# Expert choice from tokens turned once: gate products in far attention, scales by way of memory

## The chip, the cores and the metric

The kernel runs on one core of a Trainium2 chip. The metric is the device time of one execution in microseconds. Engines are named as the profile does: PE (TensorE) multiplies matrices, PEld is its weight load, DVE (VectorE), ACT (ScalarE) and POOL (GpSimd) work on vectors, and SP (SyncE) issues most DMAs. [...]

## The reference, cut to what matters

The reference runs four layers on x of shape (4, 56, 56, 128). Layer 0 is neighbourhood attention with an MLP, layer 1 a convolutional recurrence, layer 2 full attention and a dense mixture of eight experts, layer 3 an attention by distance and an expert choice. The change touches layer 3:

```python
t = t + _L3_attn_ref(_ln_t(t), ...)     # attention by distance
t = t + _L3_ffn_ref(_ln_t(t), ...)      # expert choice

# inside _L3_attn_ref
scores = jnp.exp(-GAMMA * dist2)
attn = jax.nn.softmax(scores, axis=-1)
return jnp.einsum('bqk,bkd->bqd', attn, V)       # V = inputs @ Wv.T

# inside _L3_ffn_ref, E = 64 experts, K = 8 tokens for each
logits = jnp.einsum('bsd,ed->bse', x, gate_w) + gate_b
probs = jax.nn.softmax(logits, axis=1)           # over the tokens of an image
vals, idx = jax.lax.top_k(probs.transpose(0, 2, 1), K)
# the chosen tokens are gathered and pooled by their probability, go through
# two layers of their expert, and the result is added back to the chosen tokens
```

`_ln_t` subtracts each token's mean over 128 channels and divides by its deviation.

## The kernel before, in words

**Shapes.** An image has 3136 tokens. x of all four images stays in SBUF as 28 tiles of 112 tokens (P) by 128 channels. Four tiles are a group, so an image has seven groups (NG) of 448 tokens (GW).

**Layer 3's attention** (`FarAttention`, "far"). The kernel uses that the normalised tokens lie far apart, so that every score is the same and the attention adds the mean of the values to every token. For each group it normalises the tokens (`tokens`), turns them by four TensorE transposes and one copy by ScalarE that also sums the channels (`turned`), forms short queries and keys (`products`, `with_norms`), and when all groups are done it adds to x the mean of the turned tokens times Wv (`mean`, `add`). A large set of small products, the bounds (L1861, reduced at L1867 on VectorE or L1873 on ScalarE), proves that the tokens are far apart. A fallback computes everything where they are not (`decide`).

**Layer 3's expert choice** (`ExpertChoice`). `pieces` and `steps` do for each image: statistics of the new x, an inverse root of the variance (`root`, on VectorE by Newton's steps), a `store` of x and of the roots to a table in memory, from which chosen tokens are gathered later; then for each group `tokens` (four normalisations), `turned` (four transposes, L208, and a copy, L2322) and `logits` (one TensorE product of the gate's weights, L2327, a copy to `taken`, and the eight largest values of each row, L2332). Then `choose` takes the top eight values and their places (L2350, L2351), starts four indirect DMAs that gather the tokens, `marked` marks the chosen places and takes the exponentials, and `gather` and `pooled` form the pooled tokens. Images 0 and 2 use the lower 64 partitions, images 1 and 3 the upper 64.

**Layer 3's experts.** `experts` streams 32 "lots" of weights, 1 MB each, through nine buffers. Sixteen rounds of four experts do `first` (L2442), `turned` (L2455, L2463, L2470) and `second` (L2476). The result of a round goes to a tile `found` (L2482) with two buffers, and from there by four small DMAs to `outs` (L2489). A lot's next load is issued by SP when its buffer is free, in program order with those DMAs. `scatter` adds the weighted results to x and stores the output.

**What sets the order.** The long part of the kernel is layer 2's attention, `Attention.run`: 175 steps for each image, each a score product (L2066), an exponential (L2073) and a value product (L2149). All other layers' work is cut into pieces with an estimated cost each, and `Paced` hands out pieces between the attention's steps, in proportion to cost; `merged` mixes two lists by their shares of cost. A piece marked `apart` is the last of its list in its step. The first image's layer 3 work runs beside the third image's attention, that of images 1 and 2 beside the fourth's. For the fourth image the mixture and far attention of group g - 1 trail the attention of group g (`trail`, tiles with the suffix "t"); its last group and its expert choice come behind all attention, in an order written out by hand at the end of `layers_of_safe_scores`. There, `beside` puts bounds between the steps. POOL and ACT share the normalisation of the last tokens.

Of the kernel before, what the change touches and what calls it, by code (L numbers as in the profile page):

```python
# [126 lines left out]
EARLY_BOUNDS = 4  # L127
NB = W // 8
# [1571 lines left out]
class FarAttention:  # L1700
# [16 lines left out]
    def __init__(self, env, ctx, flow, work):  # L1717
        self.env, self.flow, self.work = env, flow, work
        nc, ins = env.nc, env.ins
        self.cp = cp = ctx.enter_context(env.tc.tile_pool(name="d_const", bufs=1, side="right"))  # L1720
        self.small = ctx.enter_context(env.tc.tile_pool(name="d_small", bufs=2, side="right"))

        self.even = ctx.enter_context(ExitStack())
        self.held = [
            stack.enter_context(env.tc.tile_pool(name=name, bufs=1, side="right"))
            for stack, name in ((ctx, "d_odd"), (self.even, "d_even"))
        ]


        norm = work.tile([128, GW], F32, tag="xnT_m", name="norm")[:, : 2 * 129]  # L1730
        norm = norm.rearrange("p (i c) -> p i c", i=2)
        nc.sync.dma_start(norm, ins["norm_channels"])
        self.norm = cp.tile([128, 2, 128], BF16, tag="norm16", name="norm16")
        nc.vector.tensor_copy(self.norm, norm[:, :, :128])
        self.one = cp.tile([128, 2, 1], F32, tag="one16", name="one16")
        nc.vector.tensor_copy(self.one, norm[:, :, 128:129])
        self.q_w = cp.tile([128, NR, 32], F32, tag="q_w", name="q_w")
        self.k_w = cp.tile([128, 32], F32, tag="k_w", name="k_w")
        nc.gpsimd.memset(self.q_w, 0.0)
        nc.gpsimd.memset(self.k_w, 0.0)  # L1740
        self.far = cp.tile([128, 1], F32, tag="far", name="far")
        self.half = cp.tile([128, 1], F32, tag="half", name="half")


        n = B * NG * (NR * NC + 1)
        self.found = cp.tile([128, n], F32, tag="found", name="found")
        nc.gpsimd.memset(self.found, 0.0)
        self.most, self.sums = 0, n

    def weights(self):  # L1750
# [25 lines left out]
        def of_values():  # L1776
            ps = flow.one([128, 512], "w_ps")
            nc.tensor.transpose(ps[:, :C], loaded("w_v", ins["L3_attn_Wv"]), env.ident)
            self.v_w = cp.tile([128, C], F32, tag="v_w", name="v_w")
            nc.vector.tensor_copy(self.v_w, ps[:, :C])  # L1780
# [13 lines left out]
    def image(self, b, spans, places="d"):  # L1794
# [4 lines left out]
        x = env.x[b]  # L1799
        held = {"q": {}}  # L1800
        pool = self.held[1 - b % 2]

# [75 lines left out]
        def mean():  # L1878
# [5 lines left out]
                v_ps[:P, :C], total.to_broadcast([128, P]), self.v_w, start=True, stop=True  # L1884
            )
            held["v"] = v = sp.tile([P, C], F32, tag="v", name="v", bufs=1)
            nc.vector.tensor_copy(v, v_ps[:P, :C])

# [8 lines left out]
        def of(span):  # L1897
            take, norm = span_norms(env, sp, b, span, places)

            def tokens(g):  # L1900
                held["xn"] = normal(
                    env, self.work, places, b, g, norm, span, places == "t" and g == NG - 1
                )

            return [costing(1.8 * len(span), take)] + sum([
# [3 lines left out]
                    costing(1.2, lambda g=g: with_norms(g), True),  # L1909
                ]  # L1910
# [307 lines left out]
class ExpertChoice:  # L2218
# [9 lines left out]
    def __init__(self, env, ctx, flow):  # L2228
# [24 lines left out]
        ]  # L2253
        self.fold = cp.tile([2 * EC, EC], F32, tag="fold", name="fold")
        nc.gpsimd.tensor_tensor(self.fold, env.ident[:, :EC], env.ident[:, EC:], ALU.add)
        self.lots, self.at = {}, 0

# [7 lines left out]
    def pieces(self, b, places="d"):  # L2265
# [5 lines left out]
        for g in range(NG):  # L2271
# [10 lines left out]
    def steps(self, b, places, norms_of):  # L2282
# [20 lines left out]
        def root(groups):  # L2303
            of = slice(groups[0] * GT, (groups[-1] + 1) * GT)
            mean2, var = moments(env, sp, f"c{len(groups)}", st[:, of, :])
            inverse_root(env, sp, var, rs[:, of])
            nc.vector.scalar_tensor_tensor(off[:, of], mean2, -0.5, rs[:, of], ALU.mult, ALU.mult)
# [25 lines left out]

        def store(groups):
            of = slice(groups[0] * GT, (groups[-1] + 1) * GT)
            rows_of = self.rows[b].rearrange("(t p) c -> p t c", p=P)
# [54 lines left out]
        def pooled():  # L2391
# [13 lines left out]
            logits=logits, choose=choose, marked=marked, weighed=weighed, gather=gather,  # L2405
# [3 lines left out]
    def experts(self, ctx, pool, units, others=()):  # L2409
# [6 lines left out]
            self.late.tile([2 * EC, C], F32, tag=f"out{i}", name=f"out{i}", bufs=1) for i in range(2)  # L2416
# [55 lines left out]
        def second(q):  # L2472
# [8 lines left out]
            found = self.late.tile([128, C], F32, tag="found", name="found")  # L2481
# [24 lines left out]
    def scatter(self):  # L2506

        env, nc, flow = self.env, self.env.nc, self.flow
        for pair in range(2):
# [4 lines left out]
            bias = self.late.tile([2 * EC, C], F32, tag="c_bias", name="c_bias")  # L2514
# [382 lines left out]
def layers_of_safe_scores(env: Env, f, soft):  # L2897
    with ExitStack() as ctx:
# [63 lines left out]
        def chosen(b):  # L2962
            return listed("far", held["choice"].pieces(b))

        def to_mixture():
# [3 lines left out]
            held["far"] = far = FarAttention(env, right, flow, held["choice"].work)  # L2969
# [36 lines left out]
        with tc.manual_schedule(  # L3006
# [5 lines left out]
            *tail, products, with_norms = held["tails"][-1]  # L3012
# [24 lines left out]
            beside("scalar", 1)  # L3037
            of["tokens"](0), of["tokens"](1), of["turned"](0), of["logits"](0)
            of["root"](late)
            of["store"](late)  # L3040
            of["turned"](1), of["tokens"](2), of["logits"](1), of["turned"](2), of["logits"](2)
            beside("scalar", 1)
            of["tokens"](3), of["tokens"](4), of["turned"](3)
            of["tokens"](5), of["logits"](3), of["turned"](4)
            of["tokens"](6), of["logits"](4), of["turned"](5), of["logits"](5)
            of["turned"](6), of["logits"](6)
            of["choose"]()
            beside("scalar", 2)
# [3 lines left out]
            beside("both", 6)  # L3052
# [84 lines left out]
```

## Time and profile before

| | us |
|---|---|
| median of 3 runs | 2458.79 (2456.23 to 2465.73) |
| the profiled execution | 2462.98 |
| its span | 2461.2 |
| PE busy | 2337.9 (95%) |
| DVE busy | 1816.2 (74%) |
| ACT busy | 1550.7 (63%) |
| POOL busy | 293.8 (12%) |

Busy shares are means over the whole span. In the slices of the page, a digit is a share in tenths, and "PEclk" is the clock granted to TensorE. A row of the timeline gives the start in us, the duration, the engine, the line of the kernel, the operation, and output and input tiles with their sizes; an idle time before it, with what ended it, stands in brackets. Matrix products in float32 appear as two instructions each.

A few durations that matter: the transposes of a group of tokens (L208) have a median of 0.26 us for one; a gate product of a group is 0.96 us at full clock and 1.76 us at half. The exponential over a whole row of tokens in the tail (L2369) takes 2.90 us, the search for the top values' places (L2351) 3.42 us and their marking (L2363) 3.41 us.

### The profile page before, as it was taken

What the parts mean: (1) busy time and instruction counts of PE and PEld (TensorE: products, weight loads), DVE (VectorE), ACT (ScalarE), POOL (GpSimd) and SP (SyncE); (2) the same over time, 40 slices, a digit from 0 to 9 for tenths busy, and PEclk for the clock granted to TensorE, in tenths of its full rate; (3) what the DMA queues carried; (4) which work ended last, traced back from release to release, by engine and by line L of the source; (5) the groups of instructions that cost most, each with busy time, mean ns of one, the idle gap of its engine ahead of it and who ended that gap; (6) DMA issues with size and microseconds to landing.
All of it is one profiled execution on the core that took longest, in us unless ns stands there. A gap on an engine that the chain in (4) does not pass through costs nothing.

```text
span 2461.2 us, 38767 instructions
## 1 busy us (share of the span) xinstructions
PE 2337.9 (95%) x14357; PEld 1258.2 (51%) x14357; DVE 1816.2 (74%) x4816; ACT 1550.7 (63%) x3346; POOL 293.8 (12%) x578
## 2 busy tenths in 40 slices
PE   6999999999999999999999999999999998998585
PEld 4777777775455555555554444445444443433134
DVE  5666899983997958799678777854788576776554
ACT  4999889875666646676332556575545566775553
POOL 4423363320000000000000000100000001011302
PEclk9999999999999999999999999999999997998578
DMA  5100000000000000000000010000000010100676
GB/s 124 36 8 2 2 2 2 2 2 9 1 1 1 1 1 0 1 1 1 12 1 0 1 27 1 5 1 1 1 1 1 1 27 5 27 5 1 184 297 206
DMA packets 65642, 61.42 MB, mean 25 GB/s; under 512 B 17048, under 2 KB 60915, under 8 KB 61348
## 3 DMA queue, kind: packets, MB, share of 16 engines
q1 hardware_dynamic: 64932, 57.80, 8.4%
q8 instruction: 115, 1.88, 0.3%
q0 software_dynamic: 512, 1.06, 0.2%
q14 instruction: 83, 0.68, 0.1%
HBM read 45.83 MB, written 12.90 MB: 24 GB/s over the span
## 4 chain that ended last, share of the span: by engine, by line
PE 63%; DVE 6%; ACT 2%; DMA 2%; issue 2%; POOL 1%; SPq 0%; DVEq 0%; POOLq 0%; ACTq 0%
PE s_ps L2066 20%; PE o_ps L2149 20%; PE y_ps L1574 7%; PE d_ps L1861 3%; PE xT_ps L208 2%; PE g_ps L1207 2%; DMA lot<-in_L_ffn_lots 2%; PE l_ps L2327 1%; PE y_ps L2090 1%; PE z_ps L2042 1%; PE q_ps L1825 1%; DVE found L1867 1%; PE l_ps L1534 1%; ACT xn L1693 1%; DVE gated L1587 1%
## 5 line engine op out<-in xcount | busy, mean ns | idle before, releaser
L2073 ACT ACTIVATE e<-s_ps 128x448 f32<-128x448 f32 x688 | 366.5, 541 | 491.8 <-PE s_ps L2066 486.1
L2066 PE MATMUL s_ps<-zT,xnT 128*128 128x448 f32 (+1 forms) x1400 | 649.4, 554 | 0.0
L2149 PE MATMUL o_ps<-e,keep 128*128 128x448 f32 (+1 forms) x1376 | 648.5, 554 | 0.0
L2149 PEld LDWEIGHTS o_ps<-e,keep 128*128 128x128 f32 (+1 forms) x1376 | 241.7, 190 | 217.8 <-issue 217.2
L2066 PEld LDWEIGHTS s_ps<-zT,xnT 128*128 128x128 f32 (+1 forms) x1400 | 241.1, 189 | 213.9 <-issue 193.5
L1873 ACT ACTIVATE d_ps<-d_ps,half 128x448 f32<-128x448 f32 (+1 forms) x376 | 227.2, 605 | 88.0 <-PE d_ps L1861 86.3
L1867 DVE TENSOR_REDUCE found<-d_ps 128x1 f32<-128x448 f32 x324 | 196.9, 619 | 77.6 <-PE d_ps L1861 75.7
L1574 PE MATMUL y_ps<-experts,xnT 128*112 128x512 f32 x448 | 217.0, 608 | 0.0
L1587 DVE TENSOR_TENSOR gated<-y_ps,gate 112x512 f32<-112x512 f32 x220 | 148.8, 686 | 35.5 <-PE y_ps L1574 33.0
L1593 DVE TENSOR_TENSOR gated<-gated 112x512 f32<-112x512 f32 x330 | 151.8, 467 | 3.5
L1861 PE MATMUL d_ps<-q_near,k_near 32*128 32x448 bf16 (+1 forms) x700 | 135.4, 374 | 15.6 <-ACT d_ps L1873 10.0
L208 PE MATMUL xT_ps<-ident,xn 112*128 112x112 f32 x672 | 117.8, 283 | 34.1 <-ACT xn L1693 26.0
L208 PEld LDWEIGHTS xT_ps<-ident,xn 112*128 112x128 f32 x672 | 80.4, 147 | 113.5 <-ACT xn L1693 58.9
L1673 POOL TENSOR_TENSOR g_rs<-var,exponent 112x4 f32<-112x4 f32 x17 | 17.9, 1053 | 1006.3 <-DVE var L1672 895.3
L1574 PEld LDWEIGHTS y_ps<-experts,xnT 128*112 128x112 f32 x448 | 77.2, 180 | 98.9 <-issue 63.8
L1861 PEld LDWEIGHTS <-k_near 32*128 32x128 bf16 (+1 forms) x700 | 32.0, 92 | 181.2 <-issue 167.2
L1693 ACT ACTIVATE xn<-x,g_off,g_rs 112x128 f32<-112x128 f32 x220 | 93.2, 486 | 26.3 <-DVE g_off L1675 13.0
L677 DVE TENSOR_TENSOR e<-e,band 112x1792 f32<-112x1792 f32 (+3 forms) x56 | 99.9, 1788 | 10.2 <-ACT e L670 10.2
L782 PE MATMUL f_ps<-w_fc,h 128*112 128x128 f32 x896 | 104.8, 274 | 1.9 <-ACT h L773 1.6
L782 PEld LDWEIGHTS f_ps<-w_fc,h 128*112 128x112 f32 x896 | 99.8, 177 | 5.2 <-ACT h L773 4.8
L768 PE MATMUL h_ps<-zT,w_fc 128*128 128x448 f32 x224 | 88.9, 540 | 0.6 <-ACT zT L762 0.6
L670 ACT ACTIVATE e<-s_ps 112x1792 f32<-112x1792 f32 (+3 forms) x56 | 82.6, 1476 | 6.3 <-PE s_ps L661 3.3
(427 smaller groups left out, 3939.7 us busy)
## 6 DMA issues: line engine op xcount, KB each, us to landing
lot<-in_L_ffn_lots SPq DMA_DIRECT2D x32, 1024.0 KB
out_x<-x SPq DMA_DIRECT2D x28, 224.0 KB
x<-in_x SPq DMA_DIRECT2D x3, 1568.0 KB
rows<-x SPq DMA_DIRECT2D x3, 1568.0 KB
x<-in_x SPq DMA_DIRECT2D x7, 224.0 KB
parts<-in_waves SPq DMA_DIRECT2D x8, 173.0 KB
out<-found SPq DMA_DIRECT2D x60, 2.0 KB
rows<-x SPq DMA_DIRECT2D x1, 896.0 KB
```

Source lines behind the costliest of these rows:

```text
L208: self.nc.tensor.transpose(ps[:, j * P : (j + 1) * P], xn[:, j, :], self.ident[:P, :P])
L782: nc.tensor.matmul(f_ps[:, j, :], h[:, k, j * P : (j + 1) * P], w_fc2[:, k, :], start=(k == 0), stop=(k == 3),)
L1574: nc.tensor.matmul(y_ps, held["xnT"][g][:, j * P : (j + 1) * P], self.experts[:, 4 * i : 4 * i + 4, :], start=True, stop=True,)
L1587: nc.vector.tensor_tensor(gated[:, some, :], y_ps, gate[:, some].unsqueeze(2).to_broadcast([P, 4, C]), ALU.mult,)
L1593: by.tensor_tensor(gated[:, :n, :], gated[:, :n, :], gated[:, n : 2 * n, :], ALU.add)
L1693: env.nc.scalar.activation(xn[:, j, :], env.x[b][:, g * GT + j, :], AF.Identity, bias=norm["off"][:, i : i + 1], scale=norm["rs"][:, i : i ...
L1861: nc.tensor.matmul(d, held["k"][part, 128 * c : 128 * c + n], held["q"][g][part, :], start=True, stop=True,)
L1867: nc.vector.tensor_reduce(self.found[:, self.most : self.most + 1], d, AX.X, ALU.max)
L1873: nc.scalar.activation(d, d, AF.Relu, bias=self.half[:n], accum_out=self.found[:n, self.sums : self.sums + 1],)
L2066: nc.tensor.matmul(s_ps[i * n : (i + 1) * n, :GW], self.xnT[:, at : at + n], zT, start=True, stop=True,)
L2073: nc.scalar.activation(e[:n], s_ps[:n, :GW], AF.Exp)
L2149: nc.tensor.matmul(sums[:, :GW], self.keep[:n, k, :], e[:n], start=(k == 0 and g - 1 not in pairs), stop=last,)
```

## The change: what it does, and the diff

The gate's product is taken from the tokens that far attention turns, so that expert choice needs no normalised and turned tokens of its own. The gate weights are centred once (`centre`), so a token's mean drops out. For each group, far attention's new piece `logits` multiplies the turned tokens by the gate weights and each column by the token's deviation, which gives the product of the unnormalised token. When the mean of the values is known, its gate product (`moved`, one number for each expert, from a widened `v_w`) is added, and the sum is multiplied by the inverse deviation of the new x.

Both factors stand in SBUF as one number per partition (token), and are needed as rows along the free axis, on 64 partitions. `keep_scales` stores them to memory with a DMA, and `fetch_scale` reads a group's row back to 64 partitions. For the very last group's deviations and all of the last image's inverse deviations, `spread` makes the rows on TensorE instead, from a broadcast column and the identity. Empty pieces with a cost (ROWS_COME) let other work come between a store and its first use. In the last image, all additions and statistics come ahead of the first gate work, and the inverse roots are a power on GpSimd.

To make room, `outs` and `c_bias` move into other tiles and `found` has one buffer. In the hand-written order, `beside` has other counts.

```diff
+ROWS_COME = 12.0
 # FarAttention
         def of_values():
+            self.choice.centre()
...
+            nc.tensor.matmul(ps[:, C : C + EC], w_v, self.choice.gate_w, start=True, stop=True)
-            self.v_w = cp.tile([128, C], F32, tag="v_w", name="v_w")
+            self.v_w = cp.tile([128, C + EC], F32, tag="v_w", name="v_w")
...
         def mean():
...
+            m_ps = flow.one([128, 512], "m_ps")
+            nc.tensor.matmul(m_ps[rows, :1], self.v_w[:, C:], total, start=True, stop=True)
+            nc.scalar.copy(choice.moved[b // 2][rows], m_ps[rows, :1])
...
+            def deviations():
+                held["sd"] = sd = sp.tile([P, n], F32, tag=f"g_sd{n}_{places}", name="g_sd", bufs=1)
+                nc.vector.reciprocal(sd, norm["rs"])
+                if not final:
+                    choice.keep_scales(b, 0, span, sd)
             def tokens(g):
...
+                if not final:
+                    choice.fetch_scale(row[rows], b, 0, g)
+            def logits(g):
+                cols, row = slice(g * GW, (g + 1) * GW), held["row"][rows]
+                if final:
+                    ps = flow.one([128, 512], "sd_ps")
+                    choice.spread(ps, rows, held["sd"])
+                    nc.scalar.copy(row, ps[rows, :GW])
+                l_ps = flow.one([128, 512], "l_ps")[rows, :GW]
+                nc.tensor.matmul(l_ps, choice.gate_w, held["xnT"], start=True, stop=True)
+                nc.vector.tensor_tensor(raw[:, cols], l_ps, row, ALU.mult)
 # ExpertChoice
+    def keep_scales(self, b, i, span, scale):
+        self.env.nc.sync.dma_start(
+            self.scales[b][i].rearrange("g (j p) -> p (g j)", p=P)[
+                :, span[0] * GT : (span[-1] + 1) * GT
+            ].unsqueeze(2),
+            scale.unsqueeze(2),
+        )
+    def fetch_scale(self, row, b, i, g):
+        self.env.nc.sync.dma_start(row, self.scales[b][i][g].partition_broadcast(EC))
+    def spread(self, ps, rows, scale):
+        for j in range(GT):
+            self.env.nc.tensor.matmul(
+                ps[rows, j * P : (j + 1) * P], scale[:, j : j + 1].to_broadcast([P, EC]),
+                self.env.ident[:P, :P], start=True, stop=True,
+            )
     # pieces: instead of tokens, turned, logits
+        for g in range(NG + 1 if from_raw else 0):
+            if g == 0:
+                first.append(costing(ROWS_COME, lambda: None))
+            if g < NG:
+                first.append(costing(0.1, lambda g=g: steps["fetched"](g)))
+            if g == 0:
+                first.append(costing(ROWS_COME / 4, lambda: None))
+            if g:
+                first.append(costing(1.4, lambda g=g: steps["moved"](g - 1)))
     # steps
+            if last:
+                nc.vector.tensor_scalar(var, var, 1e-5, None, ALU.add)
+                nc.gpsimd.tensor_tensor(rs[:, of], var, env.exponent[:P, : var.shape[1]], ALU.pow)
+        def moved(g):
+            cols = slice(g * GW, (g + 1) * GW)
+            part = taken[:, cols]
+            if last:
+                ps = flow.one([128, 512], "rs_ps")
+                self.spread(ps, rows, rs[:, g * GT : (g + 1) * GT])
+                nc.vector.scalar_tensor_tensor(
+                    part, part, self.moved[b // 2][rows], ps[rows, :GW], ALU.add, ALU.mult
+                )
+            else:
+                nc.vector.scalar_tensor_tensor(
+                    part, part, self.moved[b // 2][rows], held.pop(("scale", g)), ALU.add, ALU.mult
+                )
+            nc.vector.max(held["best"][rows, g * KT : (g + 1) * KT], part)
     # second
-            found = self.late.tile([128, C], F32, tag="found", name="found")
+            found = self.late.tile([128, C], F32, tag="found", name="found", bufs=1)
 # the order by hand
             each("statistics", late)
-            beside("scalar", 1)
-            of["tokens"](0), of["tokens"](1), of["turned"](0), of["logits"](0)
             of["root"](late)
             of["store"](late)
-            of["turned"](1), of["tokens"](2), of["logits"](1), of["turned"](2), of["logits"](2)
+            logits()
             beside("scalar", 1)
-            of["tokens"](3), of["tokens"](4), of["turned"](3)
...
+            each("moved", early)
+            beside("scalar", 2)
+            each("moved", late)
             of["choose"]()
-            beside("scalar", 2)
+            beside("scalar", 4)
             products()
             of["marked"]()
             with_norms()
-            beside("both", 6)
+            beside("both", 8)
```

## The prediction

> **What bounds the kernel now.** I read the page's shares and slices first, then TensorE in windows of 20 us, then the timeline of the tail, then the waits of the DMA queue.
>
> ```profile
> span 2461.2 us, 38767 instructions
> PE 2337.9 (95%) x14357; PEld 1258.2 (51%) x14357; DVE 1816.2 (74%) x4816; ACT 1550.7 (63%) x3346; POOL 293.8 (12%) x578
> PEclk9999999999999999999999999999999997998578
> ```
>
> TensorE is the bound up to about 2245 us. Behind that its share and its clock fall together and the time is a chain through all engines. One dent lies earlier, the "7" of the clock. In windows (busy PE, PEld, DVE, ACT, POOL, then clock, DMA share, GB/s):
>
> ```profile
> 2020.00:2040.00 20.00, 19.66 (x79) 8.21 (x77) 7.87 (x18) 17.14 (x45) 0.00 (x0) 1.00 0.08 1
> 2040.00:2060.00 20.00, 15.62 (x47) 6.31 (x47) 9.98 (x33) 13.66 (x35) 1.01 (x1) 0.65 0.00 1
> 2060.00:2080.00 20.00, 18.55 (x42) 6.23 (x41) 13.90 (x27) 13.19 (x28) 6.21 (x10) 0.75 0.06 14
> 2080.00:2100.00 20.00, 18.50 (x49) 6.89 (x49) 17.49 (x39) 8.36 (x21) 0.74 (x3) 0.91 0.00 0
> ```
>
> TensorE's timeline there, and of a calm place of the same work, image 0's choice:
>
> ```profile
> 2045.52 1.36 PE L2327 MATMUL l_ps<-zT,gate_w 128*64 128x448 f32 x2 [0.42 <-ACT zT L2322]
> 2049.55 0.45 PE L208 MATMUL xT_ps<-ident,xn 112*128 112x112 f32 x1 [2.67 <-ACT xn L1693]
> ...
> 1502.28 0.55 PE L208 MATMUL xT_ps<-ident,xn 112*128 112x112 f32 x4
> 1502.76 0.37 PE L1861 MATMUL d_ps<-q_near,k_near 32*64 32x448 bf16 x1
> ...
> 1504.01 0.96 PE L2327 MATMUL l_ps<-zT,gate_w 128*64 128x448 f32 x2
> 1504.91 1.02 PE L2149 MATMUL o_ps<-e,keep 128*128 128x448 f32 x2
> ```
>
> In the dent the choice of image 1 stands in a heap: in the kernel's built order 63 TensorE instructions, 24 transposes and five gate products among them, lie between two score products. They wait for ScalarE's normalised tokens, and the clock falls to half. At the calm place they are strewn among attention and nothing waits.
>
> The tail, from the last image's last gate product to the first expert product:
>
> ```profile
> 2319.48 1.76 PE L2327 MATMUL l_ps<-zT,gate_w 128*64 128x448 f32 x2 [0.68 <-ACT zT L2322]
> 2322.50 0.22 DVE L2350 MAX8 top<-best 64x8 f32<-64x56 f32 x1
> 2338.26 0.15 DVE L2383 TENSOR_TENSOR share<-share,c_got 128x4 f32<-128x4 f32 x1
> 2341.98 1.94 PE L2442 MATMUL h_ps<-lot,pooledT 128*32 128x512 f32 x8
> ```
>
> **The change, part by part.** The sum is made against the profiled execution (2462.98 us, its span 2461.2 with 1.8 around it), 4.2 above the median of 2458.79.
>
> 1. Transposes of images 0 to 2: 3 x 28 go. Four take 1502.28 to 1502.76, 0.48 us of TensorE's time, elsewhere 0.38; at 0.43 for four, 21 x 0.43 = -9.0. The gate products stay (one per group, now from the attention's tokens). ScalarE loses 84 normalisations and 42 copies, which were hidden.
>
> 2. The dent. Time less busy share times clock over the three windows from 2040: 20 - 15.62x0.65 = 9.8; 20 - 18.55x0.75 = 6.1; 20 - 18.50x0.91 = 3.2; together 19.1. In the built order of the changed kernel the longest heap in the last two images is 19 instructions, and the choice's new steps have no TensorE work before their sum. So -19 if all of it goes. Against it stand new waits. VectorE gets, for each of 21 groups, a product (0.69 at L1587's nearest row) and a sum with product (0.62, L2377's row). Over 1820 to 2240 its windows sum to 309 of 420 us, 73%; the 14 sums, 7 products there and the trail's 6 make it 77%. It also waits for rows: a row goes to memory and back, two transfers of 2.5 us (median to landing of the rows' stores), while only some 12 VectorE instructions (0.3 us each in these windows) stand between the root and its first use: 5.0 - 3.6, some 1.5 to 2 us, five times. SP's later stores and fetches queue behind that wait, all with a reader a group later. Bounds of it: nothing (23% of VectorE is free), or 10 us and another dip of 19. I take +6, nearer to nothing, since image 0's choice shows TensorE waiting for nothing at 18 of 20 us of VectorE. Together -13.
>
> 3. The last image's products for groups 0 to 5 move from the tail into attention, where TensorE is the bound: 1504.01 to 1504.91 is 0.9 each, 6 x 0.9 = +5.4. Their stores and fetches have a group of some 60 us each. The sixth's VectorE product, 0.7, lies ahead of the tail: +0.7. The mean's new product with one column and its copy are off the path.
>
> 4. The tail up to the top values. Until 2290.3 (three groups added and measured) nothing changes. Then, from before's rows: moments 1.9, late statistics 16 x 0.22 = 3.5, moments 1.0, last group's product 0.7: VectorE is free for sums at 2297.4. GpSimd's power takes 1.0 behind its additions (end 2291.8): early scales at 2293.4, late at 2297.8. TensorE's spread of a group, four products of 112 columns each, is not in the trace. L2327 streams the same 448 columns: 1.76 at this clock. Early ones 2293.4 + 3 x 1.76 = 2298.7; two pieces of bounds (four products) 1.3; late ones 4 x 1.76, to 2307.0; last sum 0.68 and maxima 0.64; top at 2308.4 instead of 2322.5: -14.1. Bounds: where the four products do not overlap, 0.77 each (x_total's row), 3.1 a group: -4.8. Where TensorE is at full clock, VectorE's 7 x 1.32 from 2297.4: -15.9. Here the Trainium skill ("TensorE: Matmul & The Clock Gate", Part 1: The HAM clock gate) speaks: about 3.4 us of sustained work bring the full clock. The spreads are such work, so by the rule -15.9; by the row (0.50 throughout 2280 to 2344, and 0.50 too from 2050 to 2058 with TensorE busy 7.81 of 8) -14.1. I take the row.
>
> 5. From the top to the experts: before 2338.26 - 2322.50 = 15.8. Two more pieces for both engines are two reductions, +1.2. ScalarE's two further pieces end as the marks do (2316), hidden; bare they cost 0.8 each. The gather waits for the rows' stores on GpSimd, whose DMA ends at 2315, the queue being full of lots:
>
> ```profile
> 2312.00:2316.00 4.00, 2.86 (x7) 0.95 (x6) 1.09 (x2) 2.31 (x5) 0.88 (x2) 0.50 0.99 64
> 2316.00:2320.00 4.00, 3.22 (x7) 1.24 (x8) 0.64 (x1) 1.11 (x3) 0.00 (x0) 0.50 0.00 0
> ```
>
> Gathers from 2315.5, four in 5.2 and 2 to land: 2322.7, ahead of VectorE at 2308.4 + 17.0 = 2325.4. So it no longer has 12 us of cover but 2.7. Experts begin 14.1 - 1.2 = 12.9 earlier. The first nine lots are there since 2303, so all behind moves: -12.9.
>
> 6. "found" gets one buffer instead of two: VectorE's copy of a round now waits until the last round's four transfers have landed, and the next bias addition stands behind it. SP's waits and the last copies before:
>
> ```profile
> SPq L2489 <- DMA lot<-in_L_ffn_lots: 23.4, 15, 2.1
> ...
> 2415.00 0.29 DVE L2482 COPY found<-o_ps 128x128 f32<-128x128 f32 x1 [0.91 <-PE o_ps L2476]
> 2418.65 0.29 DVE L2482 COPY found<-o_ps 128x128 f32<-128x128 f32 x1
> 2421.36 0.28 DVE L2482 COPY found<-o_ps 128x128 f32<-128x128 f32 x1
> 2423.96 0.29 DVE L2482 COPY found<-o_ps 128x128 f32<-128x128 f32 x1 [1.26 <-PE o_ps L2476]
> ```
>
> While lots stream, seven rounds (2363.24 to 2410.07) take 6.7 us each, by DMA, and SP is held by landed lots already: nothing. In the last three rounds nothing streams: copy 0.3, semaphores 0.2, three issues of 0.54, landing 2.5 make 4.7 a round, 14.1 instead of 8.96: +5.1. Bounds: 0 and the slow rival below.
>
> Sum: -9.0 - 13 + 5.4 + 0.7 - 12.9 + 5.1 = -23.7. 2463.0 - 23.7 = 2439.3 profiled; less 4.2, a median of 2435.
>
> **The rivals.** (a) The dent moves instead of going: ScalarE still has far attention's seven groups within 13 attention steps[...]. For it speaks that the dip came from such a wait; against it the shorter heaps. Without the -13: 2448. (b) Slower: the single "found". If its transfers land only behind the two lots requested ahead of them (2 x 2.65, from 1 MB at some 395 GB/s), a round is 4.7 + 5.3 = 10.0 instead of 6.7, 13 times: +43, in place of the 5.1: 2473. It decides from 1.8 us a round. SP's wait for lots speaks for it; against it, that two lots requested in the last round keep the DMA fed meanwhile. (c) Rows come late in several places and the clock dips once more: +20, 2455. (d) All goes well: no new waits, full clock in the tail: -6 - 1.8, 2427. (e) That the DMA stores hide the tail's gain: the gather would have to start 2.7 later than reckoned; only some us of it, inside the range.
>
> **How the numbers follow.** Forecast 0.45, (a) 0.20, (b) 0.10, (c) 0.10, (d) 0.15. The likeliest one's own range is 2428 to 2445 (bounds of 4 and 6). 2424 to 2457 leaves out (b) and some 5 in 100 more. 0.5% is 12.3 us, about what a measurement can tell: below 2446.5 lie the forecast, (d) and two fifths of (a), 0.67; above 2471.1 (b), 0.10 and a little; the rest 0.22.
>
> **What would show it.** Step 2: clock 1.0 in all windows from 1400 to 2240, no wait of TensorE over 2 us there; a dent anywhere is (a) or (c). Step 1 and 3: attention's end some 16 us earlier. Step 4: the top values 23 us after the first addition to x (2285.4 to 2322.5 now, 37); a group's spread 1.8 us. Step 5: gathers not the last thing the share waits for. Step 6: copies of found 4.7 apart at the end and not over 7 in the middle. A round near 10 us, or a second clock dip, would make it wrong.

## The result, and the profile after

The changed kernel takes 2518.62 us (median of 4 runs, 2516.18 to 2521.87) where the kernel before took 2457.51 in the same comparison: 1.0242 of it, with an interval of 1.0216 to 1.0268. The forecast was 2435 and its range ended at 2457. The profiled execution has a span of 2520.0, 58.8 more than before. Its page:

```profile
span 2520.0 us, 38685 instructions
PE 2350.6 (93%) x14321; PEld 1258.7 (50%) x14321; DVE 1831.5 (73%) x4856; ACT 1492.6 (59%) x3203; POOL 292.5 (12%) x566
PEclk9999999999999999999999989999999998989787
```

TensorE's busy time hardly moved (2337.9 before), but its share fell and the clock has more dents. The stages say where. Starts are taken from the timelines: VectorE's first addition to x, the top values (L2350 before, L2462 after), the first expert product (L2442, L2555) and the first store of the output.

| stage, us | before | after | difference | forecast by the steps |
|---|---|---|---|---|
| start to the first addition | 2285.4 | 2351.7 | +66.3 | -15.9 (steps 1, 2 and 3) |
| first addition to top values | 37.1 | 21.3 | -15.8 | -14.1 (step 4) |
| top values to the first expert product | 19.5 | 21.2 | +1.7 | +1.2 (step 5) |
| experts, to the first output store | 88.1 | 94.5 | +6.4 | +5.1 (step 6) |
| rest | 31.1 | 31.3 | +0.2 | 0 |

The last four stages behave as forecast. The whole error, 82 us of it, lies in the long part ahead of the tail. There I added, in windows of 4 us from 1180 to the first request for lots (2279.1 and 2345.4), TensorE's busy share times its granted clock ("work", in us at full clock) and what is missing of the time ("lost"):

| | first lots | work | lost |
|---|---|---|---|
| before | 2279.1 | 1054.1 | 44.9 |
| after | 2345.4 | 1054.6 | 110.8 |

So TensorE has as much to do as before, and 66 us more are lost in waits and at half clock. Windows of the changed kernel at image 0's choice and in the place of the old dent (busy PE, PEld, DVE, ACT, POOL, then clock, DMA share, GB/s):

```profile
1488.00:1492.00 4.00, 4.00 (x14) 1.72 (x14) 3.34 (x9) 2.32 (x6) 0.00 (x0) 1.00 0.91 8
1492.00:1496.00 4.00, 2.04 (x7) 0.63 (x6) 0.00 (x0) 0.73 (x2) 0.00 (x0) 1.00 1.79 1
1496.00:1500.00 4.00, 0.00 (x0) 0.00 (x0) 0.00 (x0) 0.00 (x0) 0.00 (x0) 0.66 1.31 1
1500.00:1504.00 4.00, 0.00 (x0) 0.00 (x0) 0.00 (x0) 0.00 (x0) 0.00 (x0) 0.50 0.36 57
1504.00:1508.00 4.00, 2.46 (x4) 0.94 (x4) 3.86 (x7) 0.72 (x2) 0.00 (x0) 0.50 0.08 29
...
2060.00:2080.00 20.00, 10.71 (x39) 4.07 (x38) 3.29 (x19) 6.72 (x17) 1.01 (x1) 0.85 1.25 2
2080.00:2100.00 20.00, 13.28 (x47) 4.99 (x47) 12.57 (x33) 9.23 (x27) 0.00 (x0) 0.72 0.29 29
```

From 1496 to 1504 all five engines stand still. Up to 1500 the DMA engines are busy and move next to nothing: 1 GB/s. The timeline of the same place names the chain:

```profile
1487.65 0.18 DVE L925 SCALAR_TENSOR_TENSOR c_rs<-newton,guess 112x28 f32<-112x28 f32 x1
1487.85 0.31 SPq L2310 DMA_DIRECT2D scale<-c_rs  x1
1488.20 1.87 SPq L2450 DMA_DIRECT2D rows<-c_rs  x1
1499.19 6.09 SPq L2319 DMA_DIRECT2D scale<-scale  x3
1504.14 0.68 DVE L2438 SCALAR_TENSOR_TENSOR taken<-taken,moved,scale 64x448 f32<-64x448 f32 x1 [12.73 <-DMA scale<-scale]
1505.47 0.53 PE L1870 MATMUL d_ps<-q_near,k_near 32*128 32x448 bf16 x1 [11.43 <-DVE gated L1588]
```

The roots' store is issued at 1487.85; SP can issue the first load only at 1499.19, 11.3 us later, and the row is there at 1504.14. (A second store of single elements, that of the roots to the table of x, is under way with it.) VectorE stands before its sum for 12.73 us, and TensorE 11.43 us for a product of VectorE's (L1588) that stands behind that sum in the program and begins at 1504.74. The rows of the waits from 1200 to the tail (total us, times, longest):

```profile
DVE taken L1934 <- DMA row<-scale: 36.7, 5, 17.3
DVE taken L2438 <- DMA scale<-scale: 24.8, 2, 12.7
PE d_ps L1870 <- DVE taken L1934: 20.0, 2, 15.9
PE d_ps L1870 <- DVE gated L1588: 16.5, 5, 11.4
PE d_ps L1870 <- DVE found L1876: 12.4, 3, 8.8
```

Before, from 1400 to 2245, TensorE's longest wait for VectorE was 1.2 us:

```profile
PE d_ps L1861 <- DVE gated L1587: 2.5, 6, 1.2
```

VectorE waits 61.5 us for rows: 24.8 at two of the three choices, 36.7 at five products of far attention. Some 40 us of TensorE's waits in these rows stand behind that (20.0, 11.4 and 8.8); the other 8 or so stand behind waits for pooled tokens from GpSimd. In the windows of the table above, TensorE's idle time grew from 25.0 to 75.0 us, and what its busy time lost by a lower clock from 20.0 to 35.8. These two make the 66 us.

The tail, from the addition to the experts:

```profile
2351.69 0.69 DVE L1904 TENSOR_TENSOR x<-x,v 112x512 f32<-112x512 f32 x1
...
2358.64 2.28 POOL L2388 TENSOR_TENSOR c_rs<-var,exponent 112x12 f32<-112x12 f32 x1 [0.52 <-DVE var L2387]
2360.97 4.09 PE L2324 MATMUL rs_ps<-ident,c_rs 112*64 112x112 f32 x24 [3.17 <-POOL c_rs L2388]
...
2366.87 3.25 PE L2324 MATMUL rs_ps<-ident,c_rs 112*64 112x112 f32 x32 [0.35 <-ACT d_ps L1882]
...
2373.00 0.22 DVE L2462 MAX8 top<-best 64x8 f32<-64x56 f32 x1
...
2390.43 0.17 DVE L2495 TENSOR_TENSOR share<-share,c_got 128x4 f32<-128x4 f32 x1 [0.36 <-DMA c_got<-rows,c_at]
...
2394.16 1.94 PE L2555 MATMUL h_ps<-lot,pooledT 128*32 128x512 f32 x8
```

### The profile page after: what moved, and what is told of

The parts are those of the page before. It is cut to its first block, busy times and chain, and to the rows that moved or that the text cites. A ratio compares the mean times of both kernels' runs of the same rounds, so it can differ in the third digit from the quotient of the medians.

```text
span 2520.0 us, 38685 instructions
## 1 busy us (share of the span) xinstructions
PE 2350.6 (93%) x14321; PEld 1258.7 (50%) x14321; DVE 1831.5 (73%) x4856; ACT 1492.6 (59%) x3203; POOL 292.5 (12%) x566
## 3 DMA queue, kind: packets, MB, share of 16 engines
q1 hardware_dynamic: 90468, 63.40, 11.6%
## 4 chain that ended last, share of the span: by engine, by line
PE 57%; DVE 6%; DMA 6%; issue 3%; ACT 2%; POOL 2%; SPq 1%; DVEq 0%; POOLq 0%; ACTq 0%
PE s_ps L2101 18%; PE o_ps L2184 18%; PE y_ps L1575 7%; PE d_ps L1870 3%; PE g_ps L1208 2%; DMA scale<-g_sd 2%; PE xT_ps L209 2%; DMA out<-found 1%; DMA row<-scale 1%; DVE found L1876 1%; PE y_ps L2125 1%; PE z_ps L2077 1%; PE l_ps L1933 1%; PE l_ps L1535 1%; PE q_ps L1834 1%
## 5 line engine op out<-in xcount | busy, mean ns | idle before, releaser
L2101 PE MATMUL s_ps<-zT,xnT 128*128 128x448 f32 (+1 forms) x1400 | 660.8, 561 | 0.0
L2184 PE MATMUL o_ps<-e,keep 128*128 128x448 f32 (+1 forms) x1376 | 656.5, 559 | 0.0
L1588 DVE TENSOR_TENSOR gated<-y_ps,gate 112x512 f32<-112x512 f32 x220 | 148.6, 685 | 30.6 <-PE y_ps L1575 29.0
L1870 PEld LDWEIGHTS <-k_near 32*128 32x128 bf16 (+1 forms) x700 | 32.9, 92 | 239.9 <-issue 218.9
L1594 DVE TENSOR_TENSOR gated<-gated 112x512 f32<-112x512 f32 (+1 forms) x330 | 149.9, 463 | 2.2
L1674 POOL TENSOR_TENSOR g_rs<-var,exponent 112x4 f32<-112x4 f32 x17 | 17.3, 1017 | 1121.0 <-DVE var L1673 988.5
L209 PE MATMUL xT_ps<-ident,xn 112*128 112x112 f32 x560 | 93.3, 277 | 25.5 <-ACT xn L1694 16.9
L678 DVE TENSOR_TENSOR e<-e,band 112x1792 f32<-112x1792 f32 (+3 forms) x56 | 99.9, 1787 | 11.4 <-ACT e L671 11.4
L209 PEld LDWEIGHTS xT_ps<-ident,xn 112*128 112x128 f32 x560 | 64.6, 144 | 78.6 <-ACT xn L1694 38.2
```

Of the source, the lines that this page charges most:

```text
L209: self.nc.tensor.transpose(ps[:, j * P : (j + 1) * P], xn[:, j, :], self.ident[:P, :P])
L678: nc.vector.tensor_tensor(es, es, bands[stripes[i][1] == 0][:n].rearrange("p h r c -> p h (r c)").unsqueeze(2) .to_broadcast([n, NH, m, 8 ...
L1588: nc.vector.tensor_tensor(gated[:, some, :], y_ps, gate[:, some].unsqueeze(2).to_broadcast([P, 4, C]), ALU.mult,)
L1594: by.tensor_tensor(gated[:, :n, :], gated[:, :n, :], gated[:, n : 2 * n, :], ALU.add)
L1870: nc.tensor.matmul(d, held["k"][part, 128 * c : 128 * c + n], held["q"][g][part, :], start=True, stop=True,)
L2101: nc.tensor.matmul(s_ps[i * n : (i + 1) * n, :GW], self.xnT[:, at : at + n], zT, start=True, stop=True,)
```

## Experiments

Theory A: the stores of scales land slowly, because they consist of single 4-byte elements, and that alone makes the loss. Theory B: the order of the plan, or VectorE's additional work, makes it. Theory C: the single buffer of `found`. Theory D came up later: the place of the stores in the plan. The two measurements of stores (m_stores, m_strides) are one run each.

**Stores measured by themselves (m_stores).** In the kernel before, chains of one store (or two) and one dependent load:

```diff
+        forms = [
+            [turned("near0", N)], [turned("far0", N, 129)], [turned("line0", N, 16)],
+            [within("within0")], [lines("lines0")], [turned("few0", 7)],
+            [turned("near1", N), turned("far1", N, 129)],
...
+                nc.sync.dma_start(out, source)
+            nc.sync.dma_start(a, probe[:384].partition_broadcast(64))
```

> The kernel before, with 18 stores or pairs of stores put behind the choice of image 0, at a place where the DMA queue of SyncE has nothing else to do for 500 us. Each is followed by a load of 64 rows of 384 numbers that has to wait for it, and the next store waits for that load, so the times at which they are issued give the landing of each. Theory A (a store of single 4-byte elements is slow to land, and that is what the prediction had too small): 3136 elements at neighbouring addresses take about 10 us, two such stores together 16, 28 lines of 448 bytes about 2.5, 448 single elements about 6; a load about 4 to 5. If the neighbourhood of the addresses is what is slow, 3136 elements at 516 or 64 bytes from each other take 2.5 to 4 us; if it is the number of elements, they take 10 too. Theory B (the stores land in 2.5 us as the prediction had it, and the queue or the plan makes the rows late): all forms about 2.5 us. The time of the kernel stays that of the kernel before within 10 us.

Three of the eighteen in the timeline of SP's queue (neighbouring addresses, 516 bytes apart, lines); the distance from a store (L2294) to the load behind it (L2295) is the landing:

```profile
1190.37 0.68 SPq L2294 DMA_DIRECT2D near<-probe  x1
1208.36 0.52 SPq L2295 DMA_DIRECT2D probe<-in_x  x1
1211.17 0.63 SPq L2294 DMA_DIRECT2D far<-probe  x1
1217.06 0.47 SPq L2295 DMA_DIRECT2D probe<-in_x  x1
...
1233.92 0.36 SPq L2294 DMA_DIRECT2D lines<-probe  x1
1235.62 0.47 SPq L2295 DMA_DIRECT2D probe<-in_x  x1
```

| store (first, second time) | landing, us |
|---|---|
| 3136 single elements, neighbouring addresses | 18.0, 16.8 |
| 3136 single elements, 516 bytes apart | 5.9, 5.9 |
| 3136 single elements, 64 bytes apart | 6.8, 6.6 |
| 64 runs of 196 bytes | 1.7, 1.7 |
| 28 lines of 448 bytes | 1.7, 1.3 |
| 448 single elements, neighbouring addresses | 8.3, 8.0 |
| neighbouring and 516 apart, one behind the other | 21.8, 21.5 |
| two with neighbouring addresses | 28.4, 27.4 |
| two with 516 apart | 10.0, 10.0 |

A load took 2.7 to 2.9, once 4.3. So both count: being single elements costs about 4 us over lines, being neighbours another 11 to 12. That is more than the 10 us expected, in this shape of 64 partitions by 49 elements. Windows of half a us show where the time lies. For the second store of each kind, the DMA engines' last packets in the profile end at about 1340.5 with 516 bytes, 2.7 us before the landing at 1343.24; as neighbours they end at about 1324, 10.4 us before the landing at 1334.43. So most of what closeness costs comes behind the last packet that the profile shows. The kernel itself took 2487.72, 26 over before and not within 10: the built program put the stores at 1190 to 1440, and up to 1228 SP issues loads of attention weights among them. That these loads came late is likely, but not shown; the second half of the measurement has none of them.

**What distance is near (m_strides).** The same in the changed kernel's shape, with other distances:

```diff
+        forms = [
+            [across(f"across{s}", s)] for s in (1, 2, 4, 8, 16, 32, 129)
+        ] + [
+            [within("within2", 2)], [within("within4", 4)],
+            [across("few1", 1, 4)], [across("few16", 16, 4)],
+        ]
```

> The kernel before with stores put in as in the first measurement, now in the changed kernel's own shape, 112 partitions by 28 single elements (3136), each followed by a load of 112 rows of 384 numbers that waits for it. Elements of one partition lie 448 bytes or more from each other and neighbours come from neighbouring partitions (across), at 4, 8, 16, 32, 64, 128 and 516 bytes; or neighbours come from one partition (within), at 8 and 16 bytes. Theory A1 (stores of several partitions that fall into the same 64 bytes hinder each other): across takes about 10 us at 4 bytes, falls to about 6 at 64 and stays there; within takes about 6 at 8 and 16 bytes. Theory A2 (any write close behind another one into the same 64 bytes is slow, whoever makes it): within at 8 and 16 bytes takes as long as across at the same distance. 448 elements: 6 to 8 us at 4 bytes, 2.5 at 64. The time of the kernel is 15 to 30 us over that of the kernel before, since loads of weights queue behind the measured stores.

| 112 x 28 single elements | landing, us |
|---|---|
| neighbours from other partitions, 4 bytes apart | 12.0, 11.7 |
| 8 bytes | 8.3, 7.5 |
| 16 bytes | 6.1, 6.4 |
| 32, 64, 128 bytes | 5.5 to 5.9 |
| 516 bytes | 6.2, 6.3 |
| neighbours from one partition, 8 bytes apart | 16.5, 17.3 |
| neighbours from one partition, 16 bytes apart | 14.3, 13.6 |
| 448 elements, 4 bytes apart | 6.9, 8.0 |
| 448 elements, 64 bytes apart | 1.7, 1.8 |

A1 falls: neighbours from one partition are not faster but twice as slow as neighbours from several at the same distance. A2 has the direction (any write close to another is slow) but not the size. That writes which follow each other closely in one queue are the worst would fit; it was not tested. The kernel took 2478.95.

**The form of the store in the kernel (e_turned).**

```diff
     def keep_scales(self, b, i, span, scale, place="d"):
-        self.env.nc.sync.dma_start(
-            self.scales[b][i].rearrange("g (j p) -> p (g j)", p=P)[...].unsqueeze(2),
-            scale.unsqueeze(2),
-        )
+        nc.tensor.transpose(ps[:n, :P], scale, self.env.ident[:P, :P])
+        nc.scalar.copy(lines[:n], ps[:n, :P])
+        nc.sync.dma_start(
+            self.scales[b][i].rearrange("g (j p) -> (g j) p", p=P)[...], lines[:n],
+        )
```

The stores became pieces of their own in the plan, 4 cost units behind the root.

> The changed kernel, with one thing other: the scales are turned on TensorE and stored as lines of 448 bytes, not as single elements (12 more products of 112 columns, each 4 cost units behind the root). Theory A (trip of the stores): a trip of 16 us becomes 7, VectorE's waits for rows fall from 61 us to under 20, and with them the falls of the clock: 2518 becomes about 2445 to 2465. Theory B (the order of the plan, or VectorE's additional work, costs the time): 2505 to 2520. Theory C (the single buffer of found): no change, 2515 to 2520.

2447.15 us, 0.9937 of the kernel before (0.9921 to 0.9954). Work 1060.6 and lost 36.0 ahead of the first lots at 2276.6. SP's waits for the stores' landing, in the changed kernel

```profile
SPq L2319 <- DMA scale<-g_sd: 69.3, 9, 10.0
SPq L2319 <- DMA scale<-c_rs: 18.0, 2, 9.1
```

and in this one, with what is left of VectorE's waits for rows:

```profile
SPq L2328 <- DMA scale<-lines: 17.8, 11, 6.6
DVE taken L2449 <- DMA scale<-scale: 7.7, 3, 5.7
```

SP's wait for a store fell from 7.9 us to 1.6, and VectorE's waits for rows from 61.5 us to 7.7. Theory C and the additional work of B fall: the single buffer and that work are still there. The order of B is left.

**Two controls (e_back, e_split).** In the kernel with lines VectorE has 32, 6 and 34 instructions between the root and the choice's first sum, against 10, 9 and 13. So the order has moved along with the form. The first control keeps this order and stores single elements; the second stores single elements straight from their tiles, with the plan's pieces as in the kernel with lines.

```diff
 # e_back, against e_turned
+        nc.tensor.transpose(back_ps[:P, :n], lines[:n], self.env.ident[:n, :n])
+        nc.scalar.copy(lines[:P, :n], back_ps[:P, :n])
         nc.sync.dma_start(
-            self.scales[b][i].rearrange("g (j p) -> (g j) p", p=P)[...], lines[:n],
+            self.scales[b][i].rearrange("g (j p) -> p (g j)", p=P)[...].unsqueeze(2),
+            lines[:P, :n].unsqueeze(2),
         )
```

> A control for the kernel with lines of 448 bytes, in which the stores lie elsewhere in the plan too, so that VectorE has 32, 6 and 34 instructions between the root and the choice's first sum, where the changed kernel has 10, 9 and 13. Here the scales are turned into lines, turned back on TensorE and stored as single elements from there: the instructions of VectorE stand as in the kernel with lines (32, 6 and 34), the store is that of the changed kernel. Theory A (the store's landing): the trip is 8 us longer in each of 12 places, VectorE's waits for rows come back to 35 to 60 us, and the time is 2480 to 2510. Theory D (the place in the plan brought the gain, and not the form of the store): 2447 to 2455.

> The other control: the changed kernel with the stores of single elements straight from their tiles, as pieces of their own in the plan, 4 cost units behind the root, as in the kernel with lines. VectorE has 10, 3 and 16 instructions between the root and the choice's first sum. Theory A: as slow as the changed kernel within 15 us, 2500 to 2525. Theory D: 2447 to 2465.

e_back: 2572.95 us, 1.0456 (1.0438 to 1.0474). e_split: 2519.27 us, 1.0242 (1.0225 to 1.0259), the changed kernel's own time. So neither the new order nor the new place in the plan brings the gain without the lines: D falls, and with it what was left of B. Waits of e_back, then of e_split:

```profile
SPq L2331 <- DMA scale<-lines: 113.4, 12, 13.4
ACT xn L1695 <- DMA scale<-lines: 67.1, 8, 19.0
DVE taken L2452 <- DMA scale<-scale: 45.4, 8, 14.4
```

```profile
DVE taken L2444 <- DMA scale<-scale: 50.4, 5, 22.7
DVE taken L1937 <- DMA row<-scale: 16.8, 5, 6.1
```

With the same order of VectorE's instructions a store takes 9.5 us of SP's time (113.4 in 12) instead of 1.6, and VectorE waits 45.4 for rows instead of 7.7. e_back is beyond its expected 2510: the lines lie in the buffer of the next normalised tokens, so that ScalarE waited too, 67.1 us, which was not reckoned. So its direction counts, and its size does not. What the lines alone bring in the changed kernel's own order (10, 9 and 13) was not run; where the order with lines has only 6 instructions, VectorE still waits 5.7 us.

**More planned work between store and use (e_spaced).**

```diff
-ROWS_COME = 12.0
+ROWS_COME = 60.0
```

> The changed kernel with ROWS_COME 60 instead of 12, so that five times as much planned work stands between a store and its first use in images 0 to 2; the last image's seven spans have no such space and stay as they are. Theory A: VectorE's waits at the choice's sums (25 us, of 12.7 at the longest) go, and the falls of the clock behind them: 2518 becomes about 2475 to 2490; the waits at the last image's products (37 us) stay. Theory B: within 10 us of the changed kernel.

2495.69 us, 1.0137 (1.012 to 1.0154): 6 us over the range expected, and the waits went the other way round. The choice's waits grew from 24.8 us to 41.2, and the attention's fell to 8.6 from 36.7:

```profile
DVE taken L2438 <- DMA scale<-scale: 41.2, 5, 11.8
```

The built program tells why: VectorE's instructions between the root and the first sum are 11, 17 and 11, where they were 10, 9 and 13. The planned space is no instruction, and hardly any came into it. Why the attention's rows wait less is not shown, so the 23 us by which this kernel is faster than the changed one are luck.

**The last image's rows by TensorE (e_trailspread).**

```diff
-                if final:
+                if trailing:
                     ps = flow.one([128, 512], "sd_ps")
                     choice.spread(ps, rows, held["sd"])
```

and likewise for its stores and loads.

> The changed kernel; in the last image the scales of groups 0 to 5 no longer go to memory and back, but are spread over the rows by four products on TensorE, as the change has it for the last group alone. Images 0 to 2 keep stores and loads. Theory A (the trip of the stores): VectorE's waits at the last image's products (37 us in five waits) go, with the falls of the clock behind them (some 10), against 6 spreads of 0.9: 2518 becomes about 2465 to 2485; the choice's waits (25 us in two) stay. Theory B (VectorE's additional work and the plan's order): 2515 to 2525.

2496.8 us, 1.0132 (1.0112 to 1.0152): by the ratios 1.1% less than changed, and 12 us over the upper end of what was expected. The attention's rows wait no more, but all three choices wait for theirs, where it was two:

```profile
DVE taken L2438 <- DMA scale<-scale: 33.4, 3, 13.5
```

**All rows by TensorE (e_spreadall).**

```diff
-                if final:
-                    choice.spread(ps, rows, held["sd"])
+                    i = span.index(g) * GT
+                    choice.spread(ps, rows, held["sd"][:, i : i + GT])
...
-            if last:
+            if True:
                 ps = flow.one([128, 512], "rs_ps")
```

without any store or load of scales.

> The changed kernel with all 48 groups' scales spread on TensorE and no store or load of scales at all. Theory A: no wait for rows is left anywhere; the price is 47 more spreads of some 0.9 on TensorE, which is the bound: 2447 (lines, above) plus 38 for the 42 groups of images 0 to 2, plus 5 for the last image, less some 8 of waits that the lines still have: 2475 to 2490, slower than the kernel before but faster than the changed one. Theory B: VectorE's and TensorE's work is the same or more, 2515 to 2560.

2489.81 us, 1.0114 (1.0093 to 1.0134). Lost 35.9 as with lines, work 1099.3 instead of 1054.6: 44.7 for 48 additional spreads (27 and 21; the expectation counted 47), 0.93 each. With neither stores of scales nor waits for rows, the time is what the work says.

**The single found (e_found1).**

```diff
-            found = self.late.tile([128, C], F32, tag="found", name="found")
+            found = self.late.tile([128, C], F32, tag="found", name="found", bufs=1)
```

in the kernel before, and nothing else.

> The kernel before with one buffer for found instead of two, and nothing else. The prediction's step 6: the last three rounds take 4.7 us each and the ones in the middle nothing more: plus 5, about 2463. Its rival (b): 10 us in each round, plus 43, 2500.

2464.29 us against 2461.54, 1.0016 (1.0006 to 1.0025): +2.7. VectorE waits 35.6 us for `found`'s transfers in 13 rounds, most of it in the middle of the stream of lots, where that costs little.

**The last image alone (e_lastonly).**

```diff
-            return listed("far", held["choice"].pieces(b, from_raw=True))
+            return listed("far", held["choice"].pieces(b))
...
+            if not trailing:
+                return [costing(1.8 * len(span), take)] + sum([
...
```

> Images 0 to 2 as in the kernel before (normalised tokens, transposes and gate products behind the additions, no moved logits), the last image, the tail and the single found buffer as changed, the scales stored as lines of 448 bytes. It tells the prediction's steps 3 to 6 from 1 and 2. By its numbers: products in attention plus 6.1, tail and experts less 12.9, found plus 2.7 (as measured alone): 2461.5 becomes about 2457 (2452 to 2461). If the tail's gain is nothing: 2470. If the transposes and the dent (steps 1 and 2) bring nothing, it is as fast as the kernel with lines, 2447.

2458.73 us, 0.9988 (0.9978 to 0.9998), where 2457 was worked out. In its profile the stage ahead of the additions ends 5.8 later than before (step 3: 6.1), the tail takes 21.6.

**A version that beats both (e_best).**

```diff
+            if q % 2:
+                found = self.late.tile([128, C], F32, tag="found", name="found", bufs=1)
+            else:
+                found = self.work.tile([128, GW], F32, tag="xnT_d", name="found", bufs=1)[:, :C]
...
+        if i:
+            lines = self.small.tile([2 * EC, KT // 2, C + 1], F32, tag="c_got", name="lines", bufs=1)
```

> The kernel with lines of 448 bytes, and two more changes: found has two places again (every second one lies in a buffer of the attention's tokens that is free by then), and the choice's lines lie in the buffer of the gathered rows, so that no normalisation waits for their store. By the single found's price (2.7) and ScalarE's waits for the lines (5 us in five, half of them hidden): 2447 becomes 2440 to 2446, 0.991 to 0.994 of the kernel before.

2443.7 us, 0.9926 of the kernel before (0.9911 to 0.9941). Its experts take 85.9 us from the first product to the first output store, against 94.5 in the changed kernel, 92.6 in the kernel with lines and 88.1 before. That it is faster than the kernel with lines is not clear by the times: the intervals overlap.

## Why the prediction was wrong, by its own steps

**Step 2 failed, in the price of the waits: "a row goes to memory and back, two transfers of 2.5 us (median to landing of the rows' stores)".** The chain stood there: the trip, the 12 VectorE instructions of 3.6 us that cover it, SP's queue behind it. At image 0's choice the cover was right: VectorE comes to its sum at 1491.41 (1504.14 less 12.73), 3.6 us behind the store. The trip was 16.3 us, 11.3 for the store and 5.0 for the load, and not 5.0. The 2.5 came from the wrong row. In the kernel before, the view of the tile `rows` gives one landing for all that touches the tile (the first line here). The view of the DMA issues shows that it belongs to the gathers; the stores of the roots have only their size:

```profile
DMA to landing us min/median/max: 2.5/2.5/3.4
...
c_got<-rows,c_at POOLq DMA_INDIRECT x16, 2.5
...
rows<-c_rs SPq DMA_DIRECT2D x3, 12.2 KB
```

No row of before showed how long a store of single elements takes to land, and the step should have priced it as an operation that is not in the trace. A page of the Trainium skill spoke against the change here and was not weighed: "DMA: Bandwidth & Descriptors", Rules for kernel authors, has it that a last dimension that is not contiguous becomes one descriptor for each element and is to be rearranged. The runs agree: 12 us for 3136 single elements in the changed kernel's layout, 1.3 to 1.7 for the same kind of scales as 28 lines. The page gives no price for neighbours. Even the step's upper bound, 10 us and another dip of 19, is far under the 66 us lost.

**Step 3 failed too, in the cover that it gave the last image: "Their stores and fetches have a group of some 60 us each".** That put these waits at nothing, as step 2 did with "all with a reader a group later". But a group's store and its product are pieces of the same group, with no empty piece between them. In four of the six groups VectorE comes to the product 4.7 to 8.8 us behind the store, and waits 7.6, 17.3, 6.0 and 2.0 us: 32.9 of the 61.5, more than at the choices. The longest:

```profile
2062.52 0.31 SPq L2310 DMA_DIRECT2D scale<-g_sd  x1
2062.88 0.48 SPq L2310 DMA_DIRECT2D scale<-c_rs  x1
2063.41 1.86 SPq L2450 DMA_DIRECT2D rows<-c_rs  x1
2069.26 10.02 SPq L2319 DMA_DIRECT2D row<-scale  x1
```

The store of this group's 448 elements is issued at 2062.52 and its load 6.7 us later; VectorE stands from 2068.61 to 2085.94. The load, issued behind two stores of 3136 single elements for image 1's choice, takes 16.7 us, where a load took 5.0 at image 0's choice; so the trips seem to delay each other as well. Without the last image's trips the kernel is 1.1% faster than the changed one (e_trailspread). The step's own sum held where the stores are lines and the trips short: 5.8 against 6.1 (e_lastonly). That is partly luck, since TensorE's work rose by 9.0 us there, not 5.4, and 3.1 less were lost.

**The other half of step 2**, that the dent of 19 goes, is half right. With lines, the four windows that fall short from 2020 to 2140 lose 11 in its place (20 less busy share times clock: 2.1, 4.5, 1.7, 2.8). TensorE waits there 1.2 us at 2066 for the last image's normalised tokens; they wait for a copy behind VectorE's search for places (3.42 us). That is rival (a), in a small form. Its reason is not borne out: in the kernel before, the clock stands at 0.50 from 2046 on, and the wait of 2.67 us that was to have brought the dip begins at 2046.88.

**Step 1**: 9.0 for 84 transposes was too much. Work is 0.5 more than before, though 5.4 of gate products and the columns of the mean came in: by this estimate 5 to 6 went with the transposes. Steps 1 and 2 together, with lines, are the difference from e_lastonly to e_turned: 11.6 by the medians, 8.3 up to the first lots in the profiles, and not 22.

**Step 4** held: 15.8 against 14.1, in each kernel with the new tail (21.3 to 21.6 us from first addition to top values). Two of its terms were off and made up for each other. GpSimd's powers were under-priced, 2.28 and 2.90 us instead of 1.0. But four groups of late spreads took 3.25 us, 0.81 each, not 1.76: the granted clock was 0.97 from 2364 to 2368 and 1.00 to 2372. The rule of the Trainium skill that the step weighed and did not take ("TensorE: Matmul & The Clock Gate", Part 1: The HAM clock gate) gave 15.9 and the row 14.1. Here the rule was nearer.

**Step 5** held: +1.7 against 1.2. But the gathers are now what the share waits for last, if only by 0.36 us: the cover of 2.7 that was reckoned is used up.

**Step 6**: +5.1 forecast; +2.7 alone in the kernel before, +6.4 in the stage after the change. Its reason was partly wrong: the last three copies lie 3.7, 3.7 and 3.6 us apart and not 4.7, which is 2.0 more than before; the other 4 us come in the middle of the stream, where the step had nothing.

**The rivals.** (c) named the right mechanism, "Rows come late in several places and the clock dips once more", and priced it at 20 where it cost some 80 against the forecast; its size goes with the same price of 2.5 us. (b), 10 us a round, did not happen.

## What to carry to other kernels

A scale that goes through memory to become a row should be turned first and stored as lines: here one transpose and one copy cut SP's wait for a store from about 8 us to 1.6 and, with the order that came with them, turned 2.4% slower into 0.6% faster. Before a wait is priced, look whether the duration in hand belongs to that very form of transfer; a landing of a gather says nothing of a store of elements. A planned pause is no cover: count the instructions that stand between in the built order, at every place where the trip is paid and not only at the first.

## What the runs showed of the hardware

Single-element stores have two prices that the traces of these kernels had not shown by themselves. For 3136 elements, one by one from 32 to 516 bytes apart they land in 5.5 to 6.8 us, against 1.7 for runs of 196 bytes and 1.3 to 1.7 for lines of 448; at 4 bytes apart in 12 (from 64 partitions instead of 112, in 17 to 18), and where the neighbours come from one partition, in 14 to 17 even at 8 or 16 bytes. Even 448 of them take 7 to 8 us as neighbours and 1.7 to 1.8 at 64 bytes. Two stores one behind the other take 27 to 28 us as neighbours and 10 at 516 bytes. The surplus lies mostly behind the last packet in the profile: 10.4 us for neighbours from 64 partitions, 2.7 at 516 bytes. Why closeness costs so much, no run here tells.
